# Sharing TensorE's columns between the last blocks of two experts, and a new order of experts and steps, in a graph layer with a mixture of experts

## The chip, the cores and the metric

The kernel runs on one core of a Trainium2 chip, in one launch. The metric is the device time of the launch in microseconds (us). TensorE is called PE in the profile, VectorE DVE, ScalarE ACT, GpSimd POOL and SyncE SP; PEld is PE's loading of weights.

## What is computed

The input is `x`, 12500 nodes of 256 numbers, and 212500 edges from `src` to `dst`. A graph convolution is followed by a mixture of 64 experts of which each node uses two, a normalization over the nodes, and a normalization of each row:

```python
h = x * rsqrt(deg_out)[:, None]
m = segment_sum(h[src], dst) * rsqrt(deg_in)[:, None]      # sums over the edges
x1 = m @ W_gc + b_gc + (x @ W_res + b_res)
vals, idx = top_k(x1 @ Wg + bg, 2);  gates = softmax(vals)
# for each node and each of its two experts e (weights w1: 256x512, w2: 512x256):
core += gate * (gelu(x1 @ w1[e] + b1[e]) @ w2[e] + b2[e])
y = x1 + core
y = (y - mean(y, 0)) * rsqrt(var(y, 0) + eps) * gamma + beta
out = layernorm(x + y)
```

Everything is float32.

## The kernel before

The kernel has four stages. Up to about 400 us of the profiled execution it counts degrees and lays out the edges. Then come the sums over the edges in 1416 rows (`row`): for each row POOL gathers 128 rows of `h` by an indirect DMA (L938) and PE multiplies them with a one-hot matrix (L952). Between the rows run chains of steps for groups of two tiles of 128 nodes, defined in `nodes`: `square_root`, `scales`, `scale`, `turn_x`, `turned`, the dense layer (L1167), `best` (the two best experts, L1190 to L1212), `exponential`, `gates`, `ranks` (place of the node in the expert's list) and for each tile and choice `entries` (DVE, L1286 to L1295) and `enter` (PE, L1305), which write the node into the tables of the experts. A step puts its follower into a heap with `later(t, f, k)`, which runs it `k * lag_at(t)` rows after row `t`; `lag_at` falls from 11 to 1 as the last row comes near. All engines run in the order written here. The last chain has three tiles (`last`) and starts after the last row (`MC` is the number of rows).

The third stage, the experts, runs from about 2551 to 3437 us. `TOKENS` gives each place in the order of the experts by size its capacity in units of 16 nodes. The order is the smallest expert (place 63), then places 0 to 62. Each is cut into parts of at most four blocks of 128 nodes, 83 parts with 241 blocks in all. The last block of an expert, its tail, holds 16 to 128 nodes. For part `q`:

- `begin(q)` starts three parts ahead: the weights `w` (1026 KB, by SP), one sorting of slots per expert (L1762, L1764), and for each block a gather of the nodes into `xg` (POOL, L1638). Numbers of experts are read into registers of SP and DVE four experts at a time;
- `turned(q)`: the gates (L1682), two transposes per block (L1653) into `xtp`, and a DVE copy to `xT` (L1658);
- `hidden`: 8 matmults of 128 columns of `w1` with all the part's nodes streaming (L1667), and gelu on ACT (L1671) into `h1`;
- `outputs`: for each block four matmults (L1694) whose weights are the block's columns of `h1` and whose 256 streaming columns are `w2`, into the PSUM tile `yp`; DVE adds the bias (L1699) and multiplies by the gate (L1700) into `yo`; POOL adds the rows to the nodes by an indirect DMA (L1701).

```python
for q, (i, b, m) in enumerate(parts):
    h1 = hidden(given[i][0], xT, m)
    if q + AHEAD < len(parts):
        begin(q + AHEAD)
    if q + 1 < len(parts):
        xT = turned(q + 1)
    outputs(*given[i], table(q), gate.pop(q), h1, m, f"expert{i}")
```

In this stage only PE runs in the order written; DVE, ACT, POOL and SP are ordered by a scheduler, so that gathers and scatters may pass each other. Each f32 matmult shows as two MATMUL and two LDWEIGHTS records. All tails lie at column 0 of the array; a tail of at most 32 or 64 columns uses a tile of that width.

The fourth stage, both normalizations, ends the launch.

Of the kernel before, what the change touches and what calls it, by code (L numbers as in the profile page):

```python
# [19 lines left out]
P = 128  # L20
# [76 lines left out]
def last_node(g):  # L97
# [12 lines left out]
]  # L110
RPE = CAP // P
NSLOT = E * RPE
# [9 lines left out]
def gnn_moe_kernel(  # L122
# [697 lines left out]
    with ExitStack() as stack:  # L820
# [271 lines left out]
        def nodes(t0, n, t):  # L1092

            last = n == 3
            at_row(t + 12, lambda t: fetch(t0 + n))
            v = {}
# [26 lines left out]
            def square_root(t):  # L1123
                S.activation(of("rsq_r", [P, 2])[:, :n], d_in, AF.Sqrt)
                later(t, scales)

            def scales(t):
                a = v["rsq_r"][:, :n]
                V.reciprocal(a, a)
                b = of("rsq_q", [P, 2])[:, :n]  # L1130
                V.tensor_mul(b, a, a)
                V.tensor_mul(b, b, d_in)
                V.tensor_scalar(b, b, -0.5, 1.5, op0=ALU.mult, op1=ALU.add)
                V.tensor_mul(r_in[:, t0 : t0 + n], a, b)
                if last:
                    both_done(t)
                    return
                V.tensor_mul(of("root", [P, 2])[:, :n], d_in, r_in[:, t0 : t0 + n])
                later(t, scale)

            def scale(t):
                for i in range(n):
                    S.activation(xt[:, i], xt[:, i], AF.Copy, scale=v["root"][:, i : i + 1])
                later(t, lambda t: hold(t, turn_x))

            def turn_x(t):
                v["q"] = ps2.tile([P, 4 * P], F32, name="q")
                q = v["q"].rearrange("p (i k n) -> p i k n", i=2, k=2)
                for i in range(n):
                    for k in range(2):  # L1150
                        T.transpose(q[:, i, k], xt[:, i, k * P : (k + 1) * P], ident)
                later(t, turned)

# [9 lines left out]
            def dense(t):  # L1163
                for i in range(n):
                    a, r = (t0 + i) * P, rows(t0 + i)
                    for k in range(2):
                        T.matmul(  # L1167
                            gps[i][:r], acc2[:, k, a : a + r], wcat[:, k],
                            start=k == 0, stop=last and k == 1,
                        )  # L1170
                    for k in range(0 if last else 2):
                        T.matmul(
                            gps[i][:r], v["xT"][:, i, k, :r], wcat[:, 2 + k],
                            start=False, stop=k == 1,
                        )
                if last:
                    both_done(t)
                else:
                    later(t, best)

            def both_done(t):
                v["done"] = v.get("done", 0) + 1
                if v["done"] == 2:
                    later(t, best)

            def best(t):
# [15 lines left out]
                V.tensor_sub(of("less", [P, 2])[:, :n], top[:, :n, 1], top[:, :n, 0])  # L1202
                later(t, exponential)
                ix = of("ix", [P, 2, 2])
# [14 lines left out]
            def exponential(t):  # L1219
                S.activation(v["less"][:, :n], v["less"][:, :n], AF.Exp)  # L1220
                later(t, gates)

# [13 lines left out]
            def count(t):  # L1236
                both = v["both"]
                for i in range(n):
                    r = rows(t0 + i)
                    T.matmul(pps[i][:r, 0], before[:r, :r], both[:r, i], start=True, stop=True)  # L1240
                    T.matmul(pps[i][:, 1], ones_b[:r], both[:r, i], start=True, stop=True)
                later(t, ranks)

# [16 lines left out]
            def codes(t):  # L1260
# [18 lines left out]
                for i in range(n):  # L1279
                    for k in range(2):  # L1280
                        later(t, lambda t, i=i, k=k: entries(i, k, t), (2 * i + k) / 2)

            def entries(i, k, t):
# [13 lines left out]
                )  # L1297
                later(t, lambda t: enter(i, k, at, vals, t))

# [15 lines left out]
            else:  # L1315
                xt = xts.pop(t0)
            later(t, square_root)

# [284 lines left out]
    with ExitStack() as stack:  # L1603
        wp = stack.enter_context(tc.tile_pool(name="w", bufs=3))
        one = stack.enter_context(tc.tile_pool(name="x_one", bufs=1))
# [3 lines left out]

        REGS = 4  # L1610

# [7 lines left out]
        def overfull():  # L1619
# [9 lines left out]
            V.tensor_copy(over_n, some)  # L1629

        def gather(at, m):

            xg = []
            for k in range(0, m, P):
                r = min(P, m - k)
                k //= P
                g = two.tile([P, D2], F32, name="xg", bufs=16)
                GP.indirect_dma_start(  # L1638
                    out=g[:r],
                    out_offset=None,  # L1640
                    in_=x2_d,
                    in_offset=bass.IndirectOffsetOnAxis(ap=at[:r, 0, k : k + 1], axis=0),
                )
                xg.append(g[:r])
            return xg

        def turn(xg):

            xtp = ps1.tile([P, 2, 4 * P], F32, name="xtp")
            for k, g in enumerate(xg):  # L1650
                r = g.shape[0]
                for c in range(2):
                    T.transpose(  # L1653
                        xtp[:, c, k * P : k * P + r], g[:, c * P : (c + 1) * P], ident[:r, :r]
                    )
            m = k * P + r
            xT = two.tile([P, 2, 4 * P], F32, name="xT")
# [29 lines left out]

        def outputs(w, bb, at, gate, h1, m, group):
            w2 = w[:, 2 * H : 2 * H + 4 * D].rearrange("p (c d) -> p c d", d=D)
            for k in range(-(-m // P)):  # L1690
                r = min(P, m - k * P)
                yp = ps2.tile([P, D], F32, name="yp")
                for j in range(4):
                    T.matmul(  # L1694
                        yp[:r], h1[:, j, k * P : k * P + r], w2[:, j],
                        start=j == 0, stop=j == 3,
                    )
                yo = two.tile([P, D], F32, name="yo", bufs=6)
                V.tensor_add(yo[:r], yp[:r], bb[:r])  # L1699
                V.tensor_scalar_mul(yo[:r], yo[:r], gate[:r, k : k + 1])  # L1700
                st = GP.indirect_dma_start(  # L1701
                    out=z_d,
                    out_offset=bass.IndirectOffsetOnAxis(
                        ap=at[:r, 1, k : k + 1], axis=0
                    ),
                    in_=yo[:r],
                    in_offset=None,
                    compute_op=ALU.add,
                )
                if group:  # L1710
                    tc.declare_no_dep(st.ins, group=group, reason="no node has an expert twice")
                    tc.add_to_no_dep_group(group, st.ins)


        parts = []
        for i in [E - 1, *range(E - 1)]:
            n = -(-TOKENS[i] * TU // P)
            k = -(-n // 4)
            b = 0
            for j in range(k):  # L1720
                m = (n - b + k - j - 1) // (k - j)
                parts.append((i, b, min(m * P, TOKENS[i] * TU - b * P)))
                b += m
        AHEAD = 3
        xg, given = {}, {}

        def begin(q):
            i, b, m = parts[q]
            if b == 0:
                k = 0 if i == E - 1 else i % REGS  # L1730
                if k == 0:
                    n = 1 if i == E - 1 else min(REGS, E - 1 - i)
                    _, regs = nc.values_load_multi_w_load_instructions(
# [12 lines left out]
                    )  # L1746
                    given["regs"] = regs, columns
                regs, columns = given["regs"]
                columns_of[i] = columns[k]
                sort_slots(i, 0)  # L1750
                if q >= AHEAD:
                    sort_slots(i, 1)
                given[i] = load(regs[k])
            xg[q] = gather(table(q), m)

        columns_of = {}

# [12 lines left out]
        def turned(q):  # L1770
            i, b, m = parts[q]
            gate[q] = gates_of(xg[q], snd_sorted[:, i * RPE + b : i * RPE + b + 4])
            return turn(xg.pop(q))

        gate = {}
        snd_sorted = one.tile([P, NSLOT], F32)
        with tc.manual_schedule(engines={mybir.EngineType.PE}):
# [7 lines left out]
            for q, (i, b, m) in enumerate(parts):  # L1785
# [4 lines left out]
                h1 = hidden(given[i][0], xT, m)  # L1790
                if q + AHEAD < len(parts):
                    begin(q + AHEAD)
                if q + 1 < len(parts):
                    xT = turned(q + 1)
                outputs(*given[i], table(q), gate.pop(q), h1, m, f"expert{i}")
                if q == 16:
                    overfull()


        with tc.If(nc.values_load(over_n[0:1, 0:1]) > 0):  # L1800
            for a in range(NT):
                r = rows(a)
                again = two.tile([P, D], F32, name="yo", bufs=6)
                nc.sync.dma_start(again[:r], x2_d[a * P : a * P + r, :D])
                nc.sync.dma_start(z_d[a * P : a * P + r], again[:r])
            with tc.For_i(0, E, 1) as e:
# [5 lines left out]
                for b in range(0, RPE, 4):  # L1812
                    ab = at[:, :, b : b + 4]
                    g = gather(ab, 4 * P)
                    gb = gates_of(g, second[:, b : b + 4])
                    outputs(w, bb, ab, gb, hidden(w, turn(g), 4 * P), 4 * P, None)

# [193 lines left out]
```

## Time and profile before

| | |
|---|---|
| time, median of 3 runs | 3605.96 us (3599.64 to 3620.2) |
| the profiled execution | 3578.72 us |
| its span | 3576.8 us |
| mean granted TensorE clock | 0.829 |
| busy: PE, DVE, ACT, POOL | 2531.0, 1800.6, 798.8, 2175.5 us |
| experts | about 2551 to 3437 us |

Times in the rows below are from the start of the span. A row of the timeline gives the start, the length, engine, line, operation, result and operands, shapes and the number of records merged into it; in brackets stands the idle time before it and what ended it. A row of a group gives the number of records, the busy time and the mean ns of one, and then the idle time of the engine ahead of them. A matmult's length overlaps the next one's, so the spacing of starts tells what one costs.

### The profile page before, as it was taken

The page shows a single profiled execution, that of the slowest core. Times are in us where ns is not written, and L with a number is a line of the kernel's source. Part 1 is how long each engine was busy: PE and PEld are TensorE (multiplying, and loading weights), DVE is VectorE, ACT ScalarE, POOL GpSimd, SP SyncE. Part 2 cuts the span into 40 slices and gives each one's busy share as a digit, 9 for nine tenths or more (in the row PEclk, how much of TensorE's full clock was granted, in tenths as well). Part 3 has the DMA queues.
Part 4 walks back from the last instruction along what each step waited for, and adds up shares of the span by engine and source line. Part 5 has one row for each costly group of instructions (what it writes and reads, how often), then busy time and mean ns, then how long its engine had stood idle before and what let it go on. Part 6 is the DMA issues. An engine that isn't in the chain of part 4 may idle for free. (4 is left out here: it accounts for less than half of the span.)

```text
span 3576.8 us, 40049 instructions
## 1 busy us (share of the span) xinstructions
PE 2531.0 (71%) x11797; PEld 1893.4 (53%) x11797; DVE 1800.6 (50%) x7368; ACT 798.8 (22%) x1975; POOL 2175.5 (61%) x2095
## 2 busy tenths in 40 slices
PE   2526075566776667676766666677699999999966
PEld 2415043455555555554555444454377876677856
DVE  3729454355555465655555435467543333333358
ACT  2416301122111122212221111111111221122246
POOL 7250776666666666666666666665367777777610
PEclk6657566778887878897878777788899999999988
DMA  8450853444554555555544444444555666676764
GB/s 259 128 189 6 309 203 95 158 145 144 143 150 146 141 147 168 146 147 157 155 144 122 142 117 122 119 135 124 159 115 122 134 135 146 155 177 173 197 196 144
DMA packets 313919, 538.03 MB, mean 150 GB/s; under 512 B 47274, under 2 KB 233102, under 8 KB 305502
## 3 DMA queue, kind: packets, MB, share of 16 engines
q0 software_dynamic: 119360, 266.30, 28.9%
q1 hardware_dynamic: 180795, 256.19, 23.0%
q10 hardware_dynamic: 13539, 12.90, 1.2%
q8 instruction: 97, 1.59, 0.2%
q14 instruction: 128, 1.05, 0.1%
HBM read 431.02 MB, written 105.28 MB: 150 GB/s over the span
## 5 line engine op out<-in xcount | busy, mean ns | idle before, releaser
L938 POOL DMA_INDIRECT ring<-h_d,src_col x1416 | 1372.4, 969 | 711.8 <-issue 387.2
L952 PE MATMUL p<-ring,o 128*128 128x258 f32 x2832 | 902.0, 450 | 213.2 <-issue 89.7
L952 PEld LDWEIGHTS p<-ring,o 128*128 128x128 f32 x2832 | 600.4, 224 | 389.2 <-issue 214.9
L930 DVE TENSOR_SCALAR o<-lane,rel 128x128 f32<-128x128 f32 x1416 | 356.1, 297 | 402.7 <-remote 160.3
L1701 POOL DMA_INDIRECT z_d<-yo,tables x241 | 375.0, 1556 | 129.8 <-issue 58.0
L1694 PE MATMUL yp<-w,h 128*128 128x256 f32 (+7 forms) x1928 | 436.3, 381 | 0.8 <-DVE tables L1762 0.8
L1667 PE MATMUL hp<-xT,w 128*128 128x384 f32 (+22 forms) x1328 | 392.3, 449 | 9.4 <-issue 9.4
L1694 PEld LDWEIGHTS yp<-w,h 128*128 128x128 f32 (+7 forms) x1928 | 336.8, 179 | 71.0 <-issue 7.6
L1638 POOL DMA_INDIRECT xg<-x_d,tables x241 | 234.3, 972 | 183.7 <-PE xtp L1653 88.2
L1671 ACT ACTIVATE h<-hp,w 128x384 f32<-128x384 f32 (+21 forms) x332 | 178.7, 539 | 682.0 <-PE hp L1667 673.1
L1667 PEld LDWEIGHTS hp<-xT,w 128*128 128x128 f32 x1328 | 248.0, 192 | 134.1 <-issue 61.0
L1506 ACT ACTIVATE again<-again,factor 128x256 f32<-128x256 f32 x180 | 82.4, 501 | 670.3 <-issue 363.2
L986 ACT COPY s<-p 128x258 f32<-128x258 f32 x118 | 43.8, 371 | 814.8 <-PE p L952 450.0
L1658 DVE COPY xT<-xtp 128x672 f32<-128x672 f32 (+21 forms) x83 | 70.8, 853 | 305.6 <-PE xtp L1653 297.2
L1699 DVE TENSOR_TENSOR yo<-yp,bb 128x256 f32<-128x256 f32 (+7 forms) x241 | 102.0, 423 | 224.1 <-PE yp L1694 154.2
L285 POOL DMA_INDIRECT early<-in_x,src_col x130 | 135.0, 1038 | 102.4 <-DMA early_d<-early 56.3
L567 PE MATMUL deg<-o_hi,o_lo 128*128 128x98 bf16 x1254 | 107.3, 254 | 122.8 <-issue 83.8
L1481 PE MATMUL q<-r_out,tables 128*128 128x98 f32 x360 | 66.8, 315 | 150.4 <-DVE tables L1489 55.9
L1027 PE MATMUL q<-ident,s 128*128 128x128 f32 x236 | 58.9, 337 | 158.0 <-DVE tables L1489 67.5
L222 DVE TENSOR_TENSOR o_hi<-lane_b,hi 128x2450 bf16<-128x2450 bf16 (+1 forms) x67 | 95.1, 1419 | 145.8 <-remote 106.2
L565 ACT ACTIVATE s_lo<-lane_b,nb 128x128 bf16<-128x128 bf16 x396 | 121.8, 388 | 192.9 <-remote 126.7
L567 PEld LDWEIGHTS <-o_lo 128*128 128x128 bf16 x1254 | 87.5, 125 | 140.1 <-issue 91.2
(367 smaller groups left out, 3503.5 us busy)
## 6 DMA issues: line engine op xcount, KB each, us to landing
w<-in_wpack SPq DMA_DIRECT2D x64, 1026.0 KB
again<-early_d SPq DMA_DIRECT2D x90, 256.0 KB
ring<-h_d,src_col POOLq DMA_INDIRECT x1416
early_d<-early SPq DMA_DIRECT2D x65, 256.0 KB
tables<-h_d SPq DMA_DIRECT2D x104, 128.0 KB
acc<-acc_d SPq DMA_DIRECT2D x14, 896.0 KB
acc<-in_x SPq DMA_DIRECT2D x12, 1024.0 KB
x_d<-y SPq DMA_DIRECT2D x47, 258.0 KB
```

The lines of the kernel that those rows point to most:

```text
L285: GP.indirect_dma_start(out=t[:, c % 2], out_offset=None, in_=x, in_offset=bass.IndirectOffsetOnAxis(ap=src_col[:, MC + c : MC + c + 1], a ...
L565: S.activation(s_lo[:, i], lane_b, AF.Sign, bias=nb[:, k - k0, i : i + 1])
L567: T.matmul(deg, o_lo[:, i], o_hi[:, i], start=c + i == 0, stop=False)
L930: o_last[u] = V.tensor_scalar(o_of[u][:, j], lane, rel[:, c : c + 1], None, op0=ALU.is_equal)
L938: i = GP.indirect_dma_start(out=r[:, k, :D], out_offset=None, in_=h_d, in_offset=bass.IndirectOffsetOnAxis(ap=src_col[:, c : c + 1], axis=0),)
L952: i = T.matmul(p_of[g], o_of[v][:, n], r[:, k], start=j == 0, stop=j == GR - 1)
L1638: GP.indirect_dma_start(out=g[:r], out_offset=None, in_=x2_d, in_offset=bass.IndirectOffsetOnAxis(ap=at[:r, 0, k : k + 1], axis=0),)
L1667: T.matmul(hp[:, :m], w1[:, c, j * P : (j + 1) * P], xT[:, c, :m], start=c == 0, stop=c == 1,)
L1671: S.activation(h1[:, j, :m], hp[:, :m], AF.Gelu, bias=w[:, 2 * H + 4 * D + j : 2 * H + 4 * D + j + 1],)
L1694: T.matmul(yp[:r], h1[:, j, k * P : k * P + r], w2[:, j], start=j == 0, stop=j == 3,)
L1699: V.tensor_add(yo[:r], yp[:r], bb[:r])
L1701: st = GP.indirect_dma_start(out=z_d, out_offset=bass.IndirectOffsetOnAxis(ap=at[:r, 1, k : k + 1], axis=0), in_=yo[:r], in_offset=None, c ...
```

## The change

- 17 pairs of experts are formed whose tails fit into the array's 128 columns together: five in which both tails have 33 to 64 columns (kind 2+2, two tiles 64 wide), twelve in which one has 65 to 96 and the other at most 32 (kind 3+1, four tiles 32 wide). The first expert's tail is kept back (`kept`) and multiplied with the second's in `pair_of_outputs`: for each of the four products `j` all tiles in turn, at columns 0 and 64, or 0, 32, 64 and 96. Products in tails of pairs go from 17 x 8 = 136 to 12 x 16 + 5 x 8 = 232 matmults. The second expert's parts are reversed so that its tail comes first.
- The order of experts is 63, then the largest unit (an expert or a pair), the smallest, the next largest, and so on, and 62 last: 63, 1, 6, 61, 3, 7, 60, 5, 15, 59, ... 20, 62.
- POOL's gathers and scatters are issued in the written order (`in_order`). In a part with a pair, the pair's products come first, the first expert's scatter, then `begin` of the part three ahead, then the second's scatter, which waits for the first expert's scatters to land.
- Gathers and transposes of a tail take at least 80 rows (`WHOLE`).
- `w` gets four buffers instead of three, `yo` ten instead of six. Registers are read once per expert, except where places follow each other.
- Steps of node chains are at least two rows apart (`step`) except in the last chain; the entries of the last but one chain come at rows `MC` + 4.6 and on, behind the last row, and `enter` one row later. In the built program, the eight table products (L1305) of that chain move from between the last rows to behind the last dense layer, and its entries on DVE to ahead of the last L1190.

```diff
+SIDE, BLOCK = P // 2, P // 4
+WHOLE = SIDE + 16
+PAIR_OF = {}
+for _k in ((2, 2), (1, 3), (1, 1)):
...
+            def step(t, f, k=1):
+                at_row(t + k * (lag_at(t) if last else max(2, lag_at(t))), f)
...
-                        later(t, lambda t, i=i, k=k: entries(i, k, t), (2 * i + k) / 2)
+                        f = lambda t, i=i, k=k: entries(i, k, t)
+                        if t0 + n == END:
+                            at_row(MC + 4.6 + (2 * i + k) / 40, f)
+                        else:
+                            step(t, f, (2 * i + k) / 2)
...
-        wp = stack.enter_context(tc.tile_pool(name="w", bufs=3))
+        wp = stack.enter_context(tc.tile_pool(name="w", bufs=4))
...
-                r = min(P, m - k)
+                r = max(WHOLE, min(P, m - k))
...
+        def products(yp, r, w, h1, a, j):
+            w2 = w[:, 2 * H : 2 * H + 4 * D].rearrange("p (c d) -> p c d", d=D)
+            T.matmul(yp, h1[:, j, a : a + r], w2[:, j], start=j == 0, stop=j == 3)
...
+        def pair_of_outputs(two_of):
+            yp = ps2.tile([P, D], F32, name="yp")
+            tails = [of[5] % P for of in two_of]
+            width = SIDE if min(tails) > BLOCK and max(tails) <= SIDE else BLOCK
+            starts = [0, max(SIDE, -(-tails[0] // BLOCK) * BLOCK)]
+            for j in range(4):
+                for start, r, (w, bb, at, gate, h1, m, group) in zip(starts, tails, two_of):
+                    for k in range(0, r, width):
+                        n = min(width, r - k)
+                        products(yp[start + k : start + k + n], n, w, h1, m - r + k, j)
...
+        order = [E - 1]
+        while units:
+            order += units.pop(0)
+            if units:
+                order += units.pop()
+        order.append(E - 2)
...
-                if q + AHEAD < len(parts):
+                if q not in pair_at and q + AHEAD < len(parts):
                     begin(q + AHEAD)
                 if q + 1 < len(parts):
                     xT = turned(q + 1)
-                outputs(*given[i], table(q), gate.pop(q), h1, m, f"expert{i}")
+                mine = (*given[i], table(q), gate.pop(q), h1, m, f"expert{i}")
+                if q in pair_at:
+                    rest = pair_of_outputs([kept.pop(pair_at[q]), mine])
+                    begin(q + AHEAD)
+                if q in pair_at or q in pair_at.values():
+                    if q not in pair_at:
+                        kept[q] = mine
+                    mine = (*mine[:5], m // P * P, mine[6])
+                if q in pair_at:
+                    rest()
+                    outputs(*mine)
+                else:
+                    outputs(*mine)
```

More of the change, by code (lines that the diff above doesn't have):

```diff
@@ L1178, in dense @@
                 else:
-                    later(t, best)
+                    step(t, best)
             def both_done(t):
@@ L1183, in both_done @@
                 if v["done"] == 2:
-                    later(t, best)
+                    step(t, best)
             def best(t):
@@ L1297, in entries @@
                 )
-                later(t, lambda t: enter(i, k, at, vals, t))
+                f = lambda t: enter(i, k, at, vals, t)
+                if t0 + n == END:
+                    at_row(t + 1, f)
+                else:
+                    step(t, f)
             def enter(i, k, at, vals, t):
@@ L1316, in nodes @@
                 xt = xts.pop(t0)
-            later(t, square_root)
+            step(t, square_root)
         entered = [0]
@@ L1629, in overfull, with in_order @@
             V.tensor_copy(over_n, some)
+        issued = {"group": None, "these": [], "before": []}
+        def in_order(i, group=None):
+            if "over" in issued:
+                return
+            if group is None or group != issued["group"]:
+                issued.update(group=group, before=issued["these"], these=[])
+            for j in issued["before"]:
+                tc.add_manual_dep(
+                    i.ins, j.ins.name,
+                    mybir.DependencyInfo(
+                        mybir.DependencyClass.NoSync, mybir.DependencyReason.SCHED_ONLY
+                    ),
+                    reason="gathers and scatters are issued in this order",
+                )
+            issued["these"].append(i)
         def gather(at, m):
@@ L1693, in outputs @@
                 for j in range(4):
[L1694 to L1709, printed above, removed]
@@ L1715, in gnn_moe_kernel @@
+        units = []
+        for i in range(E - 2):
+            if i not in PAIR_OF.values():
+                units.append([i, PAIR_OF[i]] if i in PAIR_OF else [i])
+        units.sort(key=lambda u: -sum(TOKENS[i] for i in u))
+        order = [E - 1]
[4 more added lines that the diff above has]
+        order.append(E - 2)
         parts = []
-        for i in [E - 1, *range(E - 1)]:
+        for i in order:
             n = -(-TOKENS[i] * TU // P)
@@ L1728, in begin @@
             i, b, m = parts[q]
[L1729 to L1732, printed above, removed]
+            if i not in given:
+                if i not in columns_of:
+                    n = 1
+                    at = order.index(i)
+                    while n < REGS and order[at : at + n + 1] == [*range(i, i + n + 1)]:
+                        n += 1
                     _, regs = nc.values_load_multi_w_load_instructions(
```

105 lines of the change are left out of this document (79 added, 26 removed).

## The prediction

> **What bounds the kernel now.** First the slices of the page, to cut the execution into stages.
>
> ```profile
> span 3576.8 us, 40049 instructions
> ...
> PE   2526075566776667676766666677699999999966
> ...
> POOL 7250776666666666666666666665367777777610
> ```
>
> One slice is 89 us. From slice 5 to 28 no engine is full: the sums over the edges. In slices 29 to 38 PE is full while POOL stands at seven tenths: the experts. The change touches this stage, and the last microseconds of the sums ahead of it. One window gives the sizes (columns: window, length, PE, PEld, DVE, ACT, POOL busy, clock, DMA share, GB/s).
>
> ```profile
> 2582.00:3428.00 846.00, 845.18 (x3690) 629.76 (x3690) 312.38 (x951) 177.20 (x328) 585.30 (x458) 1.00 0.65 151
> ```
>
> In 846 us of experts, all at the full granted clock, PE is idle 0.8 us. So PE passes are the price of this stage: what leaves PE is gained, what is added is lost, until POOL is the bound. What one pass costs is read from the spacing of starts, not from mean durations, since matmults overlap:
>
> ```profile
> 3356.68 3.62 PE L1694 MATMUL yp<-w,h 128*128 128x256 f32 x16
> 3360.14 3.62 PE L1667 MATMUL hp<-xT,w 128*128 128x256 f32 x16
> ...
> 3363.59 0.58 PE L1653 MATMUL xtp<-ident,xg 128*128 128x128 f32 x4
> 3364.01 2.34 PE L1694 MATMUL yp<-w,h 128*128 128x256 f32 x10
> ```
>
> Sixteen records from 3356.68 to 3360.14 are 3.46 us, 0.216 us each; every f32 product is two records, so the four products of one block of output are 8 records, 1.73 us. The groups by shape, in the window from 2600 to 3430 us, show that the width of the tail does not matter:
>
> ```profile
> L1694 PE MATMUL yp<-w,h 128*128 128x256 f32 x1472 | 334.3, 381 | 0.0
> L1694 PE MATMUL yp<-w,h 128*80 128x256 f32 x104 | 24.6, 379 | 0.0
> L1694 PE MATMUL yp<-w,h 128*64 128x256 f32 x48 | 11.6, 385 | 0.0
> L1694 PE MATMUL yp<-w,h 128*48 128x256 f32 x40 | 9.6, 384 | 0.0
> L1694 PE MATMUL yp<-w,h 128*32 128x256 f32 x56 | 13.4, 382 | 0.0
> L1694 PE MATMUL yp<-w,h 128*16 128x256 f32 x40 | 9.5, 380 | 0.0
> ```
>
> A tail of 16 columns takes 380 ns a record and 8 records, as a full block takes 381. In this window 23 tails are of 64 columns or fewer (184 records by 8); with the one of the first expert they are 24. That is the waste which the change goes for.
>
> **Pairs of tails.** 17 pairs are formed: 5 of kind 2+2 (each tail a 64-wide tile) and 12 of kind 3+1 (a tail of 65 to 96 columns as three 32-wide tiles, and one of 16 or 32 as the fourth). Before, a pair costs 16 records, 3.46 us. After, a 2+2 pair has 2 tiles x 4 products x 2 records = 16 records, a 3+1 pair 4 x 4 x 2 = 32. All depends on how many run beside each other, and no row of before has two tiles in different columns, so I bound it. Best: all tiles of a product run together, 8 passes a pair, 17 x 8 x 0.216 = 29.4 us gained. Worst: none does; 2+2 costs the same, 3+1 costs 16 more, 12 x 3.46 = 41.5 us lost. Between: records start in order and the two records of one product need the same columns, so only the second record of a tile and the first of the next tile overlap; n products then take n + 1 passes: 9 for 2+2 (7 fewer, 1.51 us, x5 = 7.6 gained), 17 for 3+1 (one more, 0.22, x12 = 2.6 lost), together 5.0 gained. A second limit points to the same place. Each record needs its own weight load, and the closest spacing of load plus matmult that the trace has is that of the transposes: 0.42 us for four, 0.105 each. At that spacing 32 records are 3.4 us (nothing gained by 3+1) and 16 are 1.7 (1.75 gained by each 2+2, 8.8 in all). I take the in-order value, 5.0, since both limits give about it; the fully parallel one would need a cadence of 0.054, half of the closest seen.
>
> Whether loads hide in this mode:
>
> ```profile
> L1694 PEld LDWEIGHTS yp<-w,h 128*32 128x32 f32 x56 | 5.6, 109 | 6.8 <-issue 2.3
> ```
>
> The window above has 629.76 us of loads beside a PE that is busy 845.18 of 846, so loads run beside matmults that use the same rows and columns. [...]
>
> **Padding and mode switches.** Narrow tiles also cost at their borders. A part with an 80-wide tail against one with a narrow tail, both with six transposes and three blocks:
>
> ```profile
> 3204.89 0.74 PE L1653 MATMUL xtp<-ident,xg 128*128 128x128 f32 x6
> 3205.47 5.38 PE L1694 MATMUL yp<-w,h 128*128 128x256 f32 x24
> 3210.69 4.68 PE L1667 MATMUL hp<-xT,w 128*128 128x336 f32 x16
> ...
> 3329.51 0.82 PE L1653 MATMUL xtp<-ident,xg 128*128 128x128 f32 x6
> 3330.26 5.56 PE L1694 MATMUL yp<-w,h 128*128 128x256 f32 x24
> 3335.76 3.93 PE L1667 MATMUL hp<-xT,w 128*128 128x272 f32 x16
> ```
>
> From first transpose to next hidden layer: 5.80 against 6.25 us, so a narrow tail costs 0.45 us, which I halve between its narrow transposes and its narrow products (two borders each). After, gathers and transposes are at least 80 rows: 24 x 0.22 = 5.4 gained. Narrow products remain in 17 pairs and 2 lone tails: 19 instead of 24, 5 x 0.22 = 1.1 gained. Bounds: nothing, and 10.8 if all of it goes.
>
> **Order of the experts, POOL's order, buffers.** POOL's work, by these rows:
>
> ```profile
> 2590.29 0.98 POOL L1638 DMA_INDIRECT xg<-x_d,tables  x1 [0.30 <-issue]
> 2591.57 0.94 POOL L1638 DMA_INDIRECT xg<-x_d,tables  x1 [0.30 <-issue]
> ...
> 2597.16 1.57 POOL L1701 DMA_INDIRECT z_d<-yo,tables  x1 [0.30 <-issue]
> 2599.04 1.56 POOL L1701 DMA_INDIRECT z_d<-yo,tables  x1 [0.30 <-DVE yo L1700]
> ...
> L1701 POOL DMA_INDIRECT z_d<-yo,tables x241 | 375.0, 1556 | 129.8 <-issue 58.0
> L1638 POOL DMA_INDIRECT xg<-x_d,tables x241 | 234.3, 972 | 183.7 <-PE xtp L1653 88.2
> ```
>
> A gather every 1.28 us and a scatter every 1.88: 3.16 a block, 241 blocks, 762 us, against PE's 846. Their number does not change, nor does padding to 80 rows, as a gather's time does not go with rows in these entries. Large and small experts in turn spread the demand, so POOL stays about a tenth below PE everywhere. New is a wait: the second expert's scatters of a pair wait for the first's to land.
>
> ```profile
> 3430.93 1.53 POOL z_d L1701
> 3432.79 3.70 DMA z_d<-yo,tables
> ```
>
> That is 3.70 us. Between the two scatters the change puts the gathers of the part three ahead: with three of them 3 x 1.28 = 3.8 covers it, with two POOL waits 1.1. Queued behind the wait are the part's other scatters, and the next gathers, three parts ahead of their use. If the cover were gone 17 x 3.70 = 63 us would come to POOL, 825 in all, still under PE's 835. I cost it at nothing. The loads of registers come once an expert, some 48 more on DVE and on SP; the trace gives them no duration, the nearest row on DVE is
>
> ```profile
> L1762 DVE COPY tables<-tables 128x8 int32 x58 | 9.3, 222 | 2.0 <-issue 1.7
> ```
>
> at 0.22: 11 us on a DVE busy for 312 of 846: nothing, and 11 at worst were each on the path. The fourth w buffer and four more yo buffers only loosen waits that are not last. The first part after the first expert still has four blocks, so the gap at the start of the stage stays:
>
> ```profile
> 2567.29 3.75 PE L1694 MATMUL yp<-w,h 128*128 128x256 f32 x16
> 2579.80 8.67 PE L1667 MATMUL hp<-xT,w 128*128 128x512 f32 x16 [8.76 <-issue]
> ```
>
> 8.76 us, costed at no change, with 8.76 as the bound both ways.
>
> **End of the sums.** The steps two rows apart move the table entries of the last chain but one behind the last rows.
>
> ```profile
> 2510.39 0.95 POOL L938 DMA_INDIRECT ring<-h_d,src_col  x1 [0.30 <-issue]
> ...
> 2521.59 1.04 PE L1305 MATMUL tab<-at,vals 128*128 128x512 bf16 x2 [3.21 <-DVE vals L1291]
> 2522.41 1.07 PE L952 MATMUL p<-ring,o 128*128 128x258 f32 x2
> ...
> 2525.60 0.59 PE L1305 MATMUL tab<-at,vals 128*128 128x512 bf16 x2
> 2526.03 3.65 PE L952 MATMUL p<-ring,o 128*128 128x258 f32 x16
> ...
> 2521.01 0.35 DVE L1286 TENSOR_SCALAR at<-slots,code 128x512 bf16<-128x512 f16 x1
> ...
> 2521.66 0.35 DVE L1286 TENSOR_SCALAR at<-slots,code 128x512 bf16<-128x512 f16 x1
> ...
> 2534.03 1.01 DVE L1190 SCALAR_TENSOR_TENSOR rel<-bank,r_in,rel 128x320 f32<-128x320 f32 x2
> ```
>
> PE waits 3.21 us for an entry while the last gather was issued at 2510.39, and then gives 0.82 us to the first and 0.43 to the last of four pairs of table products, 0.62 x 4 = 2.5 us, ahead of rows that the last chain needs. Both leave: the last rows, and with them what the last chain starts from, come 5.7 us sooner. The entries' twelve DVE operations, 0.65 us for each of four entries (2521.01 to 2521.66), 2.6 us, come ahead of L1190 instead, so it starts 5.7 - 2.6 = 3.1 us sooner. The table products fall into PE's wait behind the dense layer. Bounds: 5.7 gained; 2.6 lost if another stall takes this one's place. The chains further ahead only step later, with rows to fill the time: nothing.
>
> **Sum.** -5.0 - 5.4 - 1.1 - 3.1 = -14.6 us. The profiled execution took 3578.72 us (its span and 1.9 around it), 27 under the median of 3605.96 of the three timed runs; off the execution the sum gives 3564.1, off the median 3591.4. The changed kernel's time will be a median too, so I forecast **3591**.
>
> **The rivals.** (a) The tiles run fully side by side: -29.4 - 5.4 - 1.1 - 3.1 = -39.0, 3567 us. For it: the tiles share no column and no partition of the result; against it: the 0.105 spacing. (b) Slower: tiles in different columns take turns. Place: the 12 pairs of kind 3+1; price: +41.5 - 9.6 = +31.9, 3638 us. It decides as soon as a 32-record pair takes over 4.3 us (3.46, and 9.6 / 12 = 0.8 that the rest gives back). For it: no row shows two tiles at once, and before, 16 columns cost as much as 128; against it: nothing else in the rows. [...] (c) The order on POOL stalls PE: a scatter that waits for its products holds back the gathers behind it, which today may pass it; where parts of one or two blocks follow each other the lead of three parts is short, and 17 pairs losing one scatter's cadence and landing, 1.88 + 3.70, on the path would take 17 x 5.6 = 95 us at most; a fifth of it in place of the pairs' 5.0 gives 3615. Against it: POOL's tenth in reserve.
>
> **Chances.** A measurement of this kernel can tell about 0.5%, 18 us, from no change. Forecast 0.40, of which 0.18 beyond -18 us (the 8.8 of the second limit or the larger bounds of padding and drain), 0.20 within, 0.02 slower; (a) 0.32, all faster; (b) 0.16, all slower; (c) 0.12: 0.02 faster, 0.04 same, 0.06 slower. So faster 0.52, same 0.24, slower 0.24. The range goes from (a) with the padding's and the drain's bounds (10.8 for 6.5, 5.7 for 3.1), 3560, and half of the 8.76 us gap at the start, 3556, to (b), 3638; beyond either end I leave a tenth at most. The range of the likeliest alone goes from its sum with those bounds and the second limit (-4.3 - 2.6 - 3.8, 3581) to the sum without padding and with the drain's loss (+6.5 + 5.7, 3604).
>
> **What would show it.** In the new trace: a 3+1 group of products spans 3.4 to 3.7 us in the forecast, about 1.75 in (a), 6.9 in (b); a 2+2 group 1.7 to 1.9, or 3.5 in (b); transposes of small parts at 0.58 for six instead of 0.75; the stage from the first hidden layer to the last scatter 11.5 us shorter; L1305 of the last chain but one behind L1167, and no 3.21 us stall. POOL with long waits ahead of gathers, and PE idle over 10 us between 2600 and the end of the stage, would mean (c). The forecast is wrong if the pairs span something else, or PE is not full.

## The result and the profile after

The changed kernel takes 3841.52 us (median of 6 runs, 3821.52 to 3856.95) against 3607.52 for the kernel before beside it (3595.25 to 3622.89): 1.0643 times the time before, 95% interval 1.0598 to 1.0688. 234 us were lost where 14.6 were forecast as gained. The profiled execution has a span of 3851.9 us.

The slices, the experts now being in slices 27 to 38 (the first is slice 0):

```profile
span 3851.9 us, 40290 instructions
...
PE   2534176666666766766766666667888787888776
...
POOL 6331776666666666666666666535555555555520
PEclk9756566787888878888877777888889888999898
```

PE is no longer full there, POOL fell from seven tenths to five, and the granted clock is below full. No engine took PE's place as the bound, so each must be waiting for another. Through the middle of the stage, in the window's columns as before:

```profile
2650.00:3650.00 1000.00, 804.79 (x3598) 593.77 (x3598) 274.01 (x806) 162.37 (x304) 554.28 (x439) 0.90 0.53 122
```

PE is idle for 195 of 1000 us, and what it does is done at a clock of 0.90. The stage from the experts' first transpose to the start of their last scatter grew from 873.0 to 1106.2 us (2559.8 to 3432.8, and 2602.1 to 3708.2). That is 233 us, as much as the medians lost. The two profiled executions are 275 us apart; the other 42 lie ahead of the experts, where executions of one program differ too: a_ahead4, a_late_ahead4, a_late_22 and a_late_31 below have the same program up to there and ran on one chip, and their first transposes come at 2565.9 to 2589.5. The groups by line name the wait; first DVE's gates and PE's products and hidden layers before, then DVE's gates, POOL's scatters and PE's two lines after:

```profile
L1682 DVE SCALAR_TENSOR_TENSOR gate<-snd_sorted,xg 128x1 f32<-128x1 f32 (+7 forms) x241 | 39.4, 215 | 13.7 <-DMA xg<-x_d,tables 10.9
L1694 PE MATMUL yp<-w,h 128*128 128x256 f32 (+7 forms) x1928 | 436.3, 381 | 0.8 <-DVE tables L1762 0.8
L1667 PE MATMUL hp<-xT,w 128*128 128x384 f32 (+22 forms) x1328 | 392.3, 449 | 9.4 <-issue 9.4
```

```profile
L1733 DVE SCALAR_TENSOR_TENSOR gate<-snd_sorted,xg 128x1 f32<-128x1 f32 (+3 forms) x241 | 51.6, 218 | 567.2 <-DMA xg<-x_d,tables 560.4
L1751 POOL DMA_INDIRECT z_d<-yo,tables x241 | 375.1, 1556 | 431.5 <-DVE yo L1746 358.8 <-issue 36.0 <-DVE yo L1745 17.2
L1741 PE MATMUL yp<-w,h 128*128 128x256 f32 (+5 forms) x2120 | 447.5, 401 | 138.6 <-DVE yo L1745 138.6
L1718 PE MATMUL hp<-xT,w 128*128 128x384 f32 (+21 forms) x1328 | 420.0, 473 | 71.0 <-DVE xT L1709 70.0 <-DVE gate L1733 1.0
```

DVE stands 560 us before a gate, an operation on at most 128 numbers, until a gather lands; before it was 11. POOL stands 359 us for results of DVE, and PE 209 us for DVE. One turn of this circle, on POOL and then on DVE and PE:

```profile
2969.47 0.95 POOL L1689 DMA_INDIRECT xg<-x_d,tables  x1 [0.30 <-issue]
2970.73 0.91 POOL L1689 DMA_INDIRECT xg<-x_d,tables  x1 [0.31 <-issue]
2979.91 1.62 POOL L1751 DMA_INDIRECT z_d<-yo,tables  x1 [8.27 <-DVE yo L1746]
2981.84 1.46 POOL L1751 DMA_INDIRECT z_d<-yo,tables  x1 [0.30 <-issue]
2983.60 1.01 POOL L1689 DMA_INDIRECT xg<-x_d,tables  x1 [0.30 <-PE yp L1741]
2984.91 0.97 POOL L1689 DMA_INDIRECT xg<-x_d,tables  x1 [0.30 <-issue]
2989.40 1.61 POOL L1751 DMA_INDIRECT z_d<-yo,tables  x1 [3.52 <-DVE yo L1746]
...
2978.70 0.22 DVE L1733 SCALAR_TENSOR_TENSOR gate<-snd_sorted,xg 80x1 f32<-80x1 f32 x1 [2.28 <-DMA xg<-x_d,tables]
2978.83 0.41 DVE L1745 TENSOR_TENSOR yo<-yp,bb 128x256 f32<-128x256 f32 x1
2986.49 0.22 DVE L1733 SCALAR_TENSOR_TENSOR gate<-snd_sorted,xg 128x1 f32<-128x1 f32 x1 [6.14 <-DMA xg<-x_d,tables]
2987.65 0.22 DVE L1733 SCALAR_TENSOR_TENSOR gate<-snd_sorted,xg 112x1 f32<-112x1 f32 x1 [0.94 <-DMA xg<-x_d,tables]
2988.32 0.41 DVE L1745 TENSOR_TENSOR yo<-yp,bb 128x256 f32<-128x256 f32 x1
...
2982.19 3.64 PE L1741 MATMUL yp<-w,h 128*128 128x256 f32 x16
2988.79 1.81 PE L1741 MATMUL yp<-w,h 128*128 128x256 f32 x5 [2.96 <-DVE yo L1745]
```

The last of four gathers is issued at 2970.73, the gate that needs it runs at 2978.70 (a long wait; the next one shown, 2984.91 to 2987.65, takes 2.7 us), the results behind that gate follow, and only then the scatter at 2979.91. Behind two scatters POOL issues the next gathers at 2983.60 and 2984.91, and at 2986.49 and 2987.65 DVE's gates wait for them while products lie ready in PSUM and PE waits for a free tile.

The built programs show why. DVE's order, set by the scheduler, is alike before and after: the gates of parts further on stand ahead of the copy and the results of the next part. In the changed kernel:

```
5442 L1733 TensorScalarPtr gate<-snd_sorted,xg 128x1 x2
5443 L1733 TensorScalarPtr gate<-snd_sorted,xg 80x1
5444 L1733 TensorScalarPtr gate<-snd_sorted,xg 128x1 x2
5445 L1733 TensorScalarPtr gate<-snd_sorted,xg 80x1
5446 L1709 TensorCopy xT<-xtp 128x2x480
5447 L1745 TensorTensor yo<-yp,bb 128x256
```

What changed is where POOL's gathers lie. I count for each gather its **slack**: the blocks of results that stand ahead of its gate on DVE, less the scatters that stand ahead of the gather itself on POOL. At 0, the gather is issued only once the very last result ahead of its gate is done, so DVE waits out the gathers and the landing. Free to order, the scheduler had let gathers pass scatters: mean slack 9.4 blocks. In the written order it is 0.5, and 194 of 241 gathers have 0. Counted in the order that the traces show, both means and the 194 are the same.

### The profile page after: what moved, and what is told of

Its sections match the earlier page's. It is cut to its first block, busy times and chain, and to the rows that moved or that the text cites. A ratio compares the mean times of both kernels' runs of the same rounds, so it can differ in the third digit from the quotient of the medians.

```text
span 3851.9 us, 40290 instructions
## 1 busy us (share of the span) xinstructions
PE 2575.7 (67%) x11921; PEld 1915.6 (50%) x11989; DVE 1791.9 (47%) x7368; ACT 797.3 (21%) x1975; POOL 2172.5 (56%) x2095
## 5 line engine op out<-in xcount | busy, mean ns | idle before, releaser
L973 PE MATMUL p<-ring,o 128*128 128x258 f32 x2832 | 911.4, 454 | 226.0 <-DMA ring<-h_d,src_col 105.1
L1741 PE MATMUL yp<-w,h 128*128 128x256 f32 (+5 forms) x2120 | 447.5, 401 | 138.6 <-DVE yo L1745 138.6
L1718 PE MATMUL hp<-xT,w 128*128 128x384 f32 (+21 forms) x1328 | 420.0, 473 | 71.0 <-DVE xT L1709 70.0
L1741 PEld LDWEIGHTS yp<-w,h 128*128 128x128 f32 (+4 forms) x2120 | 335.4, 179 | 219.3 <-DVE yo L1745 151.3
L1718 PEld LDWEIGHTS hp<-xT,w 128*128 128x128 f32 x1328 | 266.5, 206 | 208.1 <-DVE xT L1709 77.0
L1733 DVE SCALAR_TENSOR_TENSOR gate<-snd_sorted,xg 128x1 f32<-128x1 f32 (+3 forms) x241 | 51.6, 218 | 567.2 <-DMA xg<-x_d,tables 560.4
L1514 PEld LDWEIGHTS q<-r_out,tables 128*128 128x128 f32 x360 | 63.0, 230 | 190.4 <-issue 72.9
```

The costliest lines, as they stand in the source:

```text
L973: i = T.matmul(p_of[g], o_of[v][:, n], r[:, k], start=j == 0, stop=j == GR - 1)
L1514: T.matmul(p_r[:, i], wide[:, i * P : (i + 1) * P], r_out, start=True, stop=True)
L1718: T.matmul(hp[:, :m], w1[:, c, j * P : (j + 1) * P], xT[:, c, :m], start=c == 0, stop=c == 1,)
L1741: T.matmul(yp, h1[:, j, a : a + r], w2[:, j], start=j == 0, stop=j == 3)
```

## The experiments

Three theories: **L**, the loop just told; **P**, the pairs' own waits (the later `begin`, the second expert's scatter waiting for the first's landing); **E**, the alternation of large and small experts. Slack is worked out from the built orders. Stage is from the first transpose of the experts to the start of the last scatter in the profiled execution, gate idle is DVE's idle time ahead of gates.

| kernel | slack, blocks | time / time before (95%) | stage us | gate idle us |
|---|---|---|---|---|
| before | 9.4 | 1 | 873.0 | 13.7 |
| changed | 0.5 | 1.0643 (1.0598 to 1.0688) | 1106.2 | 567.2 |
| a_noorder | 9.9 | 0.9943 (0.9899 to 0.9986) | 871.9 | 34.0 |
| a_late | 5.5 | 0.9906 (0.9868 to 0.9943) | 856.3 | 60.8 |
| a_half | 2.6 | 1.0014 (0.9980 to 1.0047) | 875.2 | 343.5 |
| b_order | 0.0 | 1.0529 (1.0476 to 1.0583) | 1069.6 | 627.2 |
| b_late | 5.9 | 0.9982 (0.9941 to 1.0023) | 864.8 | 9.8 |
| a_late_nopairs | 5.8 | 0.9908 (0.9873 to 0.9943) | 854.7 | 8.6 |
| a_late_nopad | 5.5 | 0.9893 (0.9826 to 0.9959) | 848.8 | 49.1 |
| a_late_oldsteps | 5.5 | 0.9897 (0.9862 to 0.9931) | 851.2 | 65.8 |
| a_ahead4 | 0.7 | 1.0643 (1.0602 to 1.0684) | 1103.1 | 557.1 |
| a_late_ahead4 | 8.2 | 0.9938 (0.9916 to 0.9961) | 849.6 | 8.9 |
| a_late_22 | 5.7 | 0.9937 (0.9907 to 0.9968) | 857.2 | 41.9 |
| a_late_31 | 5.5 | 0.9936 (0.9911 to 0.9961) | 855.2 | 39.5 |

The chips differ (the kernel before took 3608, 3579 and 3601 us beside the three groups of runs), so ratios are compared, not times.

**a_noorder: POOL's order left free.**

```diff
         def in_order(i, group=None):
-            if "over" in issued:
-                return
+            return
```

> The changed kernel with POOL's gathers and scatters left to the scheduler again; pairs, padding, order of experts, buffers and steps stay. Theory L (a loop): with POOL's order fixed a gather stands right behind a scatter, and DVE's order has that gather's gate ahead of the results which the next scatters carry, so every part waits for a gather to land. Here the built order puts on average 9.9 blocks of results between the scatter ahead of a gather and the gate (0.5 in the changed kernel, 9.4 before): the stall goes and the pairs' gain shows, about 3570 us. Rival P (the pairs' own waits, the late begin and the second scatter's wait for the first to land, cost the time): those stay, still over 3800 us. Rival E (large and small experts in turn): stays, still over 3800 us.

3594.45 us, 0.9943. With the pairs' waits and the new order of experts in place the loss is gone; P and E fall. The forecast of 3570 was too low.

```profile
L1732 DVE SCALAR_TENSOR_TENSOR gate<-snd_sorted,xg 128x1 f32<-128x1 f32 (+3 forms) x241 | 40.2, 213 | 34.0 <-DMA xg<-x_d,tables 30.2 <-issue 1.5
```

**a_late: the order kept, the gates later.** The gates of part q + 1 are ordered behind the last result of part q - 1.

```diff
+            after = last_yo[0]
...
-                V.scalar_tensor_tensor(
+                i = V.scalar_tensor_tensor(
...
+                if after is not None and "over" not in issued:
+                    tc.add_manual_dep(i.ins, after.ins.name, ...NoSync, SCHED_ONLY...)
...
-            V.tensor_scalar_mul(yo[:r], yo[:r], gate[:r, k : k + 1])
+            last_yo[0] = V.tensor_scalar_mul(yo[:r], yo[:r], gate[:r, k : k + 1])
```

> The changed kernel with POOL's fixed order kept, and DVE's gates of a part ordered behind the last result of the part before the one in work. Built order: 5.5 blocks of results between the scatter ahead of a gather and its gate. Theory L: about 3570 us, as two parts are some 15 us or more, above the 10 us that four gathers and a landing take. If the fixed order is bad by itself (POOL waits for results while gathers could go): over 3700 us. Rivals P and E: over 3800 us.

3580.26 us, 0.9906: by the ratio about 34 us faster than before, a small gain, and 7% faster than the changed kernel, by moving 241 small instructions on DVE. POOL's fixed order is not bad by itself.

```profile
L1736 DVE SCALAR_TENSOR_TENSOR gate<-snd_sorted,xg 128x1 f32<-128x1 f32 (+3 forms) x241 | 41.7, 213 | 60.8 <-DMA xg<-x_d,tables 57.3 <-issue 2.9
```

**a_half: the gates one part earlier than that** (`after` is the `last_yo` of the call before).

> As the run with the gates behind the part before, but with them one part earlier: 2.6 blocks of results between the scatter ahead of a gather and its gate in the built order. Theory L: between the changed kernel and the run with 5.5 blocks, nearer to the latter: 3580 to 3650 us. Rivals P and E: over 3800 us.

3617.71 us, 1.0014, between the two and near the late one. DVE still waits 343 us for gathers, but with 2.6 blocks of slack most of that is hidden from PE, which is idle for 35 of 800 us (2620 to 3420). Idle time of DVE is thus not the loss itself; what counts is how much of it reaches PE.

**b_order: the kernel before, with POOL's order fixed and nothing else.**

```diff
+                in_order(i)
                 xg.append(g[:r])
...
                     tc.add_to_no_dep_group(group, st.ins)
+                    in_order(st, group)
```

> The kernel before with nothing but POOL's gathers and scatters held to the written order. Built order: 0.0 blocks between the scatter ahead of a gather and its gate, 237 of 241 gathers at 0 (194 in the changed kernel). Theory L: as slow as the changed kernel or slower, 3800 to 3950 us, without any pair or new order of experts. Rivals P and E: as before, 3600 us.

3802.14 us, 1.0529: one edit gives 194 of the 234 us, in the old order of experts and without a pair.

```profile
L1701 DVE SCALAR_TENSOR_TENSOR gate<-snd_sorted,xg 128x1 f32<-128x1 f32 (+7 forms) x241 | 51.5, 218 | 627.2 <-DMA xg<-x_d,tables 610.8 <-issue 13.6
```

Its slack is lower than the changed kernel's and its loss is smaller, so slack near 0 tells that there is a loss, not how large. Where the other 40 us of the changed kernel come from was not taken apart.

**b_late: b_order with the late gates.**

> The kernel before with POOL's gathers and scatters held to the written order, and DVE's gates behind the results of the part before the one in work: 5.9 blocks between the scatter ahead of a gather and its gate, against 0.0 in the run with POOL's order alone. Theory L: the 194 us that POOL's order alone cost are gone, 3600 to 3620. If the fixed order is bad by itself: 3700 or more.

3565.08 us against 3578.54, 0.9982, no measurable difference from before. The same one edit undoes it there too.

```profile
L1704 DVE SCALAR_TENSOR_TENSOR gate<-snd_sorted,xg 128x1 f32<-128x1 f32 (+7 forms) x241 | 38.2, 207 | 9.8 <-DMA xg<-x_d,tables 9.8
```

**a_ahead4: the changed kernel with a lead of four parts.**

```diff
-        AHEAD = 3
+        AHEAD = 4
...
-                g = two.tile([P, D2], F32, name="xg", bufs=16)
+                g = two.tile([P, D2], F32, name="xg", bufs=20)
```

> The changed kernel with gathers four parts ahead instead of three (20 buffers of xg, 6 of gate). In the built order DVE's gates move forward with the gathers: 0.7 blocks between the scatter ahead of a gather and its gate, 184 of 241 at 0. Theory L: no better than the changed kernel, 1.05 to 1.07 times the kernel before. Rival (the lead of three parts is too short for POOL's fixed order): most of the loss is gone, under 1.02.

3838.37 us, 1.0643: no change at all. The gates move forward with the gathers, so a longer lead in the written program gives no slack. The loss is not simply that three parts are too few.

**The pairs, the padding and the steps, with the loop out of the way.** Each takes one thing from a_late: no pairs (`for _k in ():`), no padding (`r = min(P, m - k)`), the old steps (`later` instead of `step` and `at_row`), or leaves one kind of pair.

> The kernel with late gates (two parts of slack), without pairs: each tail has its own products again; padding, the alternation of large and small experts, POOL's fixed order and the steps stay. In the trace of the late-gates kernel a pair spans 1.86 us instead of the 3.46 that its two tails took alone. Theory L with pairs fully side by side: 17 x 1.6 = 27 us slower than the late-gates kernel (3580), 3600 to 3610. If the pairs' gain is eaten by POOL's waits: the same as the late-gates kernel.

> The late-gates kernel with gathers and transposes of tails at their own number of rows instead of at least 80. By the prediction's term 5.4 us slower, 3585; if the borders of narrow transposes cost nothing, 3580.

> The late-gates kernel with the steps of the node chains as before, so that the order on PE up to the experts is that of the kernel before. By the prediction's term 3.1 us slower, 3583. The traces show 48.3 to 49.0 us from the last gather of the sums to the experts' first transpose with the new steps and 49.4 with the old ones in the same experts' neighbourhood, which would leave under 1 us, 3581. If the steps cost time further ahead (the last gather came at 2539 to 2553 us with them, 2510 and 2529 without), it is 10 to 25 us faster, 3555 to 3570.

> The late-gates kernel with the pairs of kind 2+2 alone. 5 x 1.6 = 8 us less products than without pairs, whose stage took 854.7 us: 847 if nothing eats it.

> The late-gates kernel with the pairs of kind 3+1 alone, which are 13 here. 13 x 1.6 = 21 us less products than without pairs: a stage of 834 us if nothing eats it. In the late-gates kernel the waits behind pairs lay behind those of kind 3+1; if they go with this kind, the stage is 848 to 855.

All five lie between 0.9893 and 0.9937 with intervals that overlap, a_late among them, and their stages within 848.8 to 857.2 us. (The last has 12 pairs, not the 13 that the expectation says.) So none of the three parts can be told from nothing by the time, and the expected 27 us of the pairs does not show. a_late_nopairs has no pair and gains as much as a_late. So the small gain over before does not need the pairs; whether the padding, the order of experts, the buffers or the steps give it stays open. The traces say more. A group of a 3+1 pair and one of a 2+2 pair in the changed kernel:

```profile
2656.90 1.93 PE L1741 MATMUL yp<-w,h 128*32 128x256 f32 x32
...
2784.76 1.95 PE L1741 MATMUL yp<-w,h 128*64 128x256 f32 x16
```

32 records and 16 take the same 1.9 us: the tiles run fully side by side. By the starts all 17 pairs do so (1.85 to 1.88 us to the next start), and behind 16 of the 17 DVE's first add starts within 0.11 us of the last product's end in the profile. Accordingly the lines of products are cheaper in a_late than before (436.3 us for 1928 records):

```profile
L1752 PE MATMUL yp<-w,h 128*128 128x256 f32 (+5 forms) x2120 | 411.9, 384 | 10.0 <-remote 5.1 <-DVE yo L1756 4.4 <-ACT h L1722 0.6
```

But PE's idle time in the stage is 22.2 us in a_late and 2.6 without pairs. In a_late some 10 us of it lie before transposes that wait for a gather, and some 10 before products that wait for a free tile, most of these right behind a 3+1 pair:

```profile
3040.64 0.36 PE L1705 MATMUL xtp<-ident,xg 80*128 80x80 f32 x2 [0.98 <-DMA xg<-x_d,tables]
...
3125.10 3.08 PE L1752 MATMUL yp<-w,h 128*128 128x256 f32 x8 [2.42 <-remote]
```

Of the 24 us, some 20 come back as waits. Not all of these are waits for a neighbour: the last section shows that groups of kind 3+1 themselves can end late.

**a_late_ahead4: the late gates with a lead of four parts.**

> The late-gates kernel with gathers four parts ahead: 8.2 blocks between the scatter ahead of a gather and its gate. The late-gates kernel has some 10 us of PE waiting for gathers of the part behind a pair; if these come from the lead, they go, and the experts' stage falls from 856 to 846 us, ratio to before 0.985 to 0.99; if from POOL's own rate, the stage stays.

0.9938, stage 849.6 us, between the two that were expected, the ratio above both. PE's idle time falls to 14.1 us, with no wait over 0.7 us before a transpose, and from its first transpose to its last product PE takes 838.2 us instead of 869.0 before; but the last scatter comes 11 us behind the last product, 4 before. With PE shorter, POOL's scatters lag behind it.

Four kinds of version beat both kernels: a_noorder, a_late, a_late with one part less, and a_late_ahead4, by 0.6 to 1.1%. All these intervals end below 1, but no gain is as large as 2%, and which version is best these runs cannot tell.

## Why the prediction was wrong

**The step that failed** is the paragraph on POOL's order. Its "I cost it at nothing" stands behind the pairs' second scatters, and the fixed order itself, for all 241 blocks, got no term in the sum at all. The reason given was that POOL's work (762 us, 825 with every landing) lies under PE's. That POOL is not the bound was right: it was busy 554 of 1000 us, and with its order still fixed a_late takes 0.9906. But the fixed order alone, in b_order, cost 194 us (1.0529) with DVE idle 627 us ahead of its gates. What the comparison of busy times left out is that a fixed order on one engine and a scheduled order on another make a chain, whose length goes by who stands ahead of whom and not by how busy either is. I read the built order of the changed kernel for PE and for the tables at the end of the sums, and not where DVE's gates stand; the slack of 0.5 against 9.4 was there to be counted.

**Rival (c)** held a part of it: a scatter that waits for its products holds back the gathers behind it (POOL stood 359 us for results of DVE). Three things in it were wrong. It looked for the trouble at the pairs (17 x 5.6 us, "95 us at most"), where it is in every part. It argued that the lead of three parts is short, and a_ahead4 shows that a longer lead alone changes nothing. And "POOL's tenth in reserve" was held against it, which is no argument against a chain. It had a chance of 0.12 and a price of 9 us; b_order alone cost 194.

**The pairs.** The forecast took 9 and 17 passes for in-order starts and a spacing of 0.105 us per load and matmult; 8 and 8 were measured, as in rival (a): the 17 groups took 1.85 to 1.88 us each. That only the second record of a tile overlaps the first of the next was the author's estimate, and no run shows it. The records do start in order, in the 3+1 group at 2656.90 6 to 7 ns apart within a pass and most passes 0.216 us apart, but the second record of a tile did not hold back the next tile. The row of the transposes was no bound for narrow tiles: in a 3+1 group four loads and four matmults go in 0.216 us. Nor was it the closest spacing of the trace before, where the 1254 bf16 matmults of L567, each with a load, were busy for 107.3 us, 0.086 each. The loads added nothing that shows either: that group's 32 loads of 106 to 110 ns and 32 matmults, all of 128 rows, took those 1.9 us together. But the 29.4 us of rival (a) as a gain in time did not come either: 24 us left the lines of products, and some 20 came back as waits.

**The second scatter's wait** for the first's landing, costed at nothing, was not isolated. It may be among the causes of the waits behind pairs; nothing here shows it.

**Padding and borders** were put at 6.5 us, 5.4 of it for the padding. Without pairs, with padding and late gates, PE is busy 850.5 us of its stage (853.1 less 2.6 idle) against 858.2 before (869.0 less 10.7) and 856.5 in b_late: 7.7 or 5.9 less, with the order of experts changed too. Taking the padding alone out of a_late makes PE's busy time only 1.8 us longer (830.2 to 831.9). So the sign was right and the size stays open. As a time it does not show (a_late_nopad).

**The end of the sums** was put at 3.1 us. From the last gather of the sums to the experts' first transpose the four runs with old steps take 49.4, 49.5, 51.5 and 53.2 us, the ten with new steps 48.3 to 49.1. That is about 2 us, right in kind; in the time a_late_oldsteps does not show it. The stall of 3.21 us is gone and the entries lie where the step said, in front of the last L1215:

```profile
2574.24 0.16 DVE L1159 TENSOR_TENSOR r_in<-src_col 128x3 f32<-128x3 f32 x1
2574.32 0.35 DVE L1315 TENSOR_SCALAR at<-slots,code 128x512 bf16<-128x512 f16 x1
...
2576.91 1.46 DVE L1215 SCALAR_TENSOR_TENSOR rel<-bank,r_in,rel 128x320 f32<-128x320 f32 x3
...
2577.50 1.67 PE L1338 MATMUL tab<-at,vals 128*128 128x512 bf16 x7
```

**The gap of 8.76 us** at the start, costed as unchanged, fell to 1.22 in the changed kernel and to 2.52 in b_late, but stood at 9.12 in a_noorder. So it goes with POOL's order; what closed it stays open. It is the greater part of the 8.2 us by which b_late's stage is shorter than that of the kernel before (873.0 to 864.8).

**"The forecast is wrong if ... PE is not full"** and idle of over 10 us as the sign of (c) were the right things to look for: PE was idle 210 us from its first transpose to its last product.

## What to carry to other kernels

When one engine's order is fixed by hand and another's is left to a scheduler, count in the built program, for each transfer, how much work stands between what it is queued behind and who waits for it; busy shares do not show a loop (in this one no engine was busy for more than 805 of 1000 us). A small instruction that waits on a DMA can be as dear as everything queued behind it in order: here 241 gates of 0.22 us each, put later, took the ratio from 1.0643 to 0.9906. Put it as late as its use allows. When an engine that was full becomes shorter, ask at once which neighbour takes the gain; here some 20 of 24 us came back as waits.

## What was not expected of the hardware

In the changed kernel and in b_order PE stalls, and it also works slower. In the changed kernel the granted clock in the stage was 0.90 (2650 to 3650), 1.00 before (2600 to 3400); a product's mean time rose from 381 to 401 ns and the hidden layer's (L1667, now L1718) from 449 to 473. From first transpose to last product the time grew by 235.6 us (869.0 to 1104.5). PE's idle time grew by 199.5 of it (10.7 to 210.3), and its busy time by the rest. Against kernels that do the same work without the loop, the changed kernel's PE was busy 894.3 us where a_late's was busy 830.2 (clock 0.99), and b_order's 918.0 where b_late's was busy 856.5 (clock 1.00). The clock in b_order:

```profile
2650.00:3600.00 950.00, 822.01 (x3356) 591.48 (x3355) 257.78 (x719) 160.32 (x296) 543.52 (x428) 0.95 0.54 123
```

So some 60 us come with the stalls as slower work. How much of that goes with the clock was not taken apart, and the means do not settle it: a product takes 405 ns in b_order at 0.95 against 401 in the changed kernel at 0.90, a hidden layer's matmult 458 against 473.

Of the 12 pairs of kind 3+1 in a_late, seven had DVE's first add start 0.2 to 3.6 us behind the end that the profile gives to the group's last product; behind the pairs of kind 2+2 it is 0.06 to 0.08. Neither the gathers nor a free `yo` tile explains it in their rows. The latest one, a group of 32 records and 8 of the next block:

```profile
3193.03 3.86 PE L1752 MATMUL yp<-w,h 128*32 128x256 f32 x40
...
3198.54 0.88 DVE L1756 TENSOR_TENSOR yo<-yp,bb 80x256 f32<-80x256 f32 x2 [4.55 <-remote]
3198.59 0.33 SPq L1647 DMA_DIRECT2D w<-in_wpack  x1
...
3199.57 2.47 PE L1752 MATMUL yp<-w,h 128*128 128x256 f32 x8 [2.68 <-DVE yo L1756]
```

A load of weights by SP starts within 0.05 us of that add, and it does so behind all 17 pairs of a_late. So DVE itself is not what is late: one event seems to free both, and what both can be waiting for is the pair's products, which the add reads and which use weights in a buffer that a later load fills. The starts of PE's records do not show such a delay. The delays sum to some 14 us in a_late and 15 in a_late_31, and a_late_22 has none, so they are a part of why the pairs' gain does not show. What makes a 3+1 group end late stays open.
